# Mamba scan in held order: the second layer's weights made inside the scan loop, and the gate moved ahead of the scans of its slot

## The chip, the cores and the metric

The kernel runs on one core of one Trainium2 chip. The metric is device time in microseconds (us). The kernel before takes 9756.96 us, the median of three runs (9746.79 to 9757.15).

## The reference

The model is a chain of four blocks on a tensor of 4 batches, 96 channels and 64x64 positions. Blocks 0 and 2 are the ones that the change touches, and both are the same program (`mamba_fusion`) with other weights. Each has two Mamba layers and a fusion:

```python
seq = x.reshape(b, c, L).transpose(0, 2, 1)
for i in range(NLAYERS):                       # 2 layers
    seq = seq + _mamba_block(seq, ...)         # layernorm, in_w, conv of 4 taps, silu, xproj_w,
                                               # delta, A = -exp(A_log), scan, + Dp*xc, * silu(z), out_w
...
gp = relu(x.mean((2, 3)) @ gp_w.T + gp_b)      # one vector for each batch
out = einsum('oc,bchw->bohw', fus_w, cat(mamba_out, gp)) + fus_b
# batch norm of out, + residual
```

The scan is `h[t] = dA[t] * h[t-1] + dBx[t]` for 192 inner channels and 16 states, over L = 4096 positions, with `dA = exp(delta * A)` and `dBx = delta * B * xc`; `y` sums `h * C` over the states, adds `Dp * xc`, and is multiplied by `silu(z)`. That last multiplication is called the gate here. Block 1 is a state-space block in another form (`ssd`), block 3 a ConvNeXt block (`convnext`); neither is touched.

## The kernel before, in words

`mamba_fusion` works on two batches at once (a pair). A step is one pair, one layer (`sub` 0 or 1) and one chunk of 512 positions; there are 2 pairs x 2 layers x 8 chunks = 32 steps, in that order, so the second layer's weights are first needed in the ninth step. The 2 x 192 inner channels fill three blocks of 128 partitions (j = 0, 1, 2).

`Scan.run` cuts each step into 24 groups, eight for each j, and walks them with one loop variable n. One turn of that loop is called a slot, and the slot's number within its chunk a position (0 to 23). In slot n every stage works on another group, so many slots ahead or behind: `load` is five ahead (SP issues the loads of delta, and in one group of four also of delta times x, spread over the 16 states), `spread` one ahead (TensorE writes delta times x to a PSUM tile `bs`, two buffers; in the other groups ScalarE writes the exponentials there), `decay` and `product` two ahead (exponentials on ScalarE; one product on GpSimd for one group of four), `scan` in its own slot (on VectorE: one product of 128x1024, L369, in three groups of four, and then two scans of 128x512, L374), `after` one behind (GpSimd: hc = h times C, L381; ScalarE keeps the last state), `sums` three behind (TensorE: the sum over states to one PSUM bank `py` with a single buffer, L400). `front` (`mamba_front`) prepares the next step: layernorm, convolution, projections and the softplus, cut by `yield` into small parts that run one or two in a slot (`PACE`).

After the last group of a j, its gate `close` (L408) multiplies `py` by silu(z) on VectorE. It comes four slots after that group: at position 11 for j = 0, at position 19 for j = 1, and at position 3 of the next chunk for j = 2. Until it has read `py`, the first `sums` of the next j, in the same slot, can't start. `project` and `project_rest` follow one and two slots later.

The order of the work is written by hand: at the end of each slot the instructions of every engine, SP's DMA issues too, are tied behind the previous one of that engine, so that nothing in the loop is reordered:

```python
for ins in traced[start:]:
    ...
    self.tc.add_manual_dep(ins, last[ins.engine].name, IN_ORDER, reason="order")
```

Before the loop starts, `mamba_fusion` loads and prepares: selections, the first layer's weights, the whole front of the first step, sums of x for the fusion, then the second layer's weights (`mamba_weights(..., 1, ...)`, L494 to L534) and the fusion's (L629 to L655). On SP the second layer's weights are 26 issues, 16 of them for `w_a` (L527). The fusion's part turns the second layer's output weights by the fusion's matrix on TensorE (L638 to L645, PSUM tag `mm`) and makes the vector `gb`. Those instructions stand ahead of the loop's first ones; outside the loop the order is the scheduler's.

## Time and profile before

| what | value |
|---|---|
| median of three runs | 9756.96 us |
| the profiled execution's own time | 9748.23 us |
| its span, first to last instruction | 9746.5 us |
| block 0: first scan starts, last scan ends | 88.24, 3017.34 us |
| block 2: first scan starts, last scan ends | 6225.50, 9150.70 us |
| VectorE busy in 88 to 3018 us | 2733.29 of 2930 us |
| TensorE busy there, at a mean granted clock of 0.93 | 2510.75 us |
| GpSimd busy there | 2510.97 us |
| two products 24 slots apart (position 22 of the first and second chunk) | 170.77, 262.65 us |

The profile page gives the busy time of each engine over the whole span, then the costliest groups of instructions, each with the idle time of its engine just before them and with what ended that idle time. The timeline lists instructions by start; a bracket at a line's end tells how long the engine had been idle, and who released it. Matmul rows come in pairs of records for each float32 matmul, so `x4` is the two matmuls of one slot. `PEclk` and the clock of a window are shares of TensorE's full clock. VectorE is called DVE, TensorE PE, ScalarE ACT, and GpSimd POOL in the rows.

### The profile page before, as it was taken

To read this page: it belongs to the slowest core of one execution; us is meant where nothing else is said; L and a number is where in the kernel's file an instruction comes from. 1 tells how busy PE (TensorE), PEld (TensorE's weight loads), DVE (VectorE), ACT (ScalarE), POOL (GpSimd) and SP (SyncE) were. 2 spreads that over 40 slices of the span, in tenths; PEclk is the share of its full clock that TensorE was granted. 3 is DMA by queue.
4 is the path that set the end of the run, shared out by engine and by line. 5 is a ranking of instruction groups with operands and counts; after the bars stand their busy time and mean duration, and the time that the engine had idled before them with its cause. 6 is when DMAs were issued, how large, how long until landed. Compare 5 with 4: busy or idle time off the path is not lost. (4 is left out here: it accounts for less than half of the span.)

```text
span 9746.5 us, 109952 instructions
## 1 busy us (share of the span) xinstructions
PE 8319.4 (85%) x32896; PEld 3486.3 (36%) x32896; DVE 8080.8 (83%) x10870; ACT 5536.2 (57%) x10786; POOL 6860.0 (70%) x4573
## 2 busy tenths in 40 slices
PE   7888888888887998998898999688888888888678
PEld 1222222112123676776766777212222222222122
DVE  7999999999995666666666667699999999999887
ACT  5566666566664455455555545466666666666345
POOL 6888888888885555555555555588888888888511
PEclk8999999999997999999999999799999999999789
DMA  7777787777774222222322222677787877777653
GB/s 187 202 206 204 211 216 206 205 208 201 209 211 128 66 69 85 80 70 82 88 67 77 82 66 61 159 208 195 210 215 206 213 207 197 209 209 203 168 119 84
DMA packets 813856, 1531.94 MB, mean 157 GB/s; under 512 B 126893, under 2 KB 132425, under 8 KB 809802
## 3 DMA queue, kind: packets, MB, share of 16 engines
q1 hardware_dynamic: 810186, 1519.79, 58.6%
q8 instruction: 260, 4.26, 0.2%
q10 hardware_dynamic: 3072, 5.11, 0.1%
q14 instruction: 338, 2.77, 0.1%
HBM read 1229.28 MB, written 148.50 MB: 141 GB/s over the span
## 5 line engine op out<-in xcount | busy, mean ns | idle before, releaser
L381 POOL TENSOR_TENSOR hc<-hs,bc 128x1024 f32<-128x1024 f32 x1536 | 3611.0, 2356 | 742.8 <-DVE hs L374 399.9
L374 DVE TENSOR_TENSOR_SCAN hs<-da,carry,bs 128x512 f32<-128x512 f32 x2016 | 2470.8, 1267 | 119.6 <-DVE bs L369 1.4
L343 PE MATMUL bs<-du,seldu 64*128 64x512 f32 x4608 | 1467.8, 667 | 510.1 <-DVE hs L374 505.6
L400 PE MATMUL py<-hc,selsum 128*32 128x512 f32 x6144 | 1670.7, 651 | 261.5 <-DVE xz L408 180.6
L369 DVE TENSOR_TENSOR bs<-bs,bc 128x1024 f32<-128x1024 f32 x1152 | 1406.3, 1221 | 254.1 <-PE bs L343 233.1
L111 ACT ACTIVATE da<-da,w_a 128x512 f32<-128x512 f32 x2304 | 1517.1, 710 | 0.0
L343 PEld LDWEIGHTS bs<-du,seldu 64*128 64x128 f32 x4608 | 409.9, 193 | 1484.3 <-DVE hs L374 1190.2
L351 POOL TENSOR_TENSOR du<-du,bc 128x1024 f32<-128x1024 f32 x384 | 904.7, 2356 | 50.3 <-DMA du<-dg 50.3
L1032 DVE TENSOR_SCALAR seg<-dr,dac 128x128 f32<-128x128 f32 x1536 | 637.0, 448 | 290.0 <-PE y L1077 287.7
L1048 POOL TENSOR_TENSOR seg<-seg,cb 128x384 f32<-128x384 f32 x512 | 514.9, 1007 | 476.5 <-DVE cb L1047 409.0
L374 DVE TENSOR_TENSOR_SCAN hs<-bs,carry,du 128x512 f32<-128x512 f32 x672 | 819.0, 1260 | 0.0
L205 PE MATMUL pu<-h,w_conv 96*128 96x512 f32 (+3 forms) x2048 | 796.4, 624 | 1.4 <-POOL h L179 1.4
L111 ACT ACTIVATE bs<-da,w_a 128x512 f32<-128x512 f32 x768 | 528.7, 688 | 444.9 <-DVE hs L374 431.8
L983 PE MATMUL front<-pk,sconv 128*128 128x512 f32 x1536 | 753.8, 608 | 25.6 <-ACT z L971 21.7
L400 PEld LDWEIGHTS py<-hc,selsum 128*32 128x32 f32 x6144 | 222.4, 111 | 1504.8 <-issue 924.6
L1087 POOL TENSOR_TENSOR y<-y,xs 128x192 f32<-128x192 f32 x496 | 295.1, 595 | 605.1 <-DVE y L1086 590.1
L1100 ACT ACTIVATE y<-yz 128x192 f32<-128x192 f32 x512 | 186.1, 363 | 906.3 <-DVE yz L1099 905.3
L1052 POOL TENSOR_TENSOR xs<-pre,coef 128x576 f32<-128x576 f32 x512 | 597.9, 1172 | 53.4 <-ACT pre L116 25.3
L994 PE MATMUL front<-sconv,pk 128*128 128x192 f32 x3072 | 572.5, 330 | 57.1 <-DVE pre L999 51.9
L384 ACT COPY carry<-hs 128x2 f32<-128x2 f32 x1344 | 246.7, 184 | 514.2 <-DVE hs L374 513.8
L994 PEld LDWEIGHTS front<-sconv,pk 128*128 128x128 f32 x3072 | 496.7, 190 | 89.6 <-DVE pre L999 78.7
L1077 PEld LDWEIGHTS y<-xs,seg 128*128 128x128 f32 x3072 | 442.9, 206 | 144.2 <-issue 83.9
(229 smaller groups left out, 13743.1 us busy)
## 6 DMA issues: line engine op xcount, KB each, us to landing
da<-dd SPq DMA_DIRECT2D x3072, 256.0 KB
du<-dg SPq DMA_DIRECT2D x768, 256.0 KB
dr<-rows SPq DMA_DIRECT2D x256, 384.0 KB
bc<-rows SPq DMA_DIRECT2D x256, 256.0 KB
dd<-delta SPq DMA_DIRECT2D x192, 256.0 KB
dg<-du SPq DMA_DIRECT2D x192, 256.0 KB
pk<-xn SPq DMA_DIRECT2D x128, 384.0 KB
pk<-xn SPq DMA_DIRECT2D x128, 256.0 KB
```

The source lines that it names most:

```text
L111: self.last = self.scalar.activation(out, in_, func, **kw)
L205: nc.tensor.matmul(pu[r0:r1], lhsT=wt["conv"][:kk, tap, d0:d1], rhs=h[:kk, b, ds(tap, T)], start=(tap == 0), stop=(tap == 3),)
L343: nc.tensor.matmul(g["bs"][:, i], lhsT=self.sel["du"][rows, g["half"], g["q"]], rhs=g["made"]["du"][rows, g["j"]], start=True, stop=True,)
L351: self.tc.nc.gpsimd.tensor_tensor(g["du"], g["du"], self.b_or_c(g, 0), ALU.mult)
L369: nc.vector.tensor_tensor(dbx, dbx, self.b_or_c(g, 0), ALU.mult)
L374: nc.vector.tensor_tensor_scan(hs[:, i], da[:, i], dbx[:, i], init, ALU.mult, ALU.add)
L381: nc.gpsimd.tensor_tensor(g["hc"], hs, self.b_or_c(g, 1), ALU.mult)
L400: nc.tensor.matmul(py[rows], lhsT=self.sel["sum"][:, g["q"]], rhs=g["hc"][:, i], start=(g["q"] == 0), stop=(g["q"] == NQU - 1),)
L983: nc.tensor.matmul(p, lhsT=self.conv[:, i, DI + q * DST : DI + (q + 1) * DST], rhs=pk[:, i, ds(c * T, T)], start=(i == 0), stop=(i == 2),)
L994: nc.tensor.matmul(p, lhsT=pk[:, i, ds(c * Q, Q)], rhs=self.conv[:, i, :DI], start=(i == 0), stop=(i == 2),)
L1032: nc.vector.tensor_scalar(seg[:, h], g["pair"]["dr"][:, c % 2 * NH + h], made["dac"][:, n0 + h : n0 + h + 1], 0.0, ALU.subtract, ALU.min,)
L1052: nc.gpsimd.tensor_tensor(xs, x.to_broadcast([P, 3, NH, HD]), coef.to_broadcast([P, 3, NH, HD]), ALU.mult)
```

## The change

Three things are moved; nothing is computed otherwise.

- The second layer's and the fusion's weights are made by a generator, `other_weights`, handed to `run` as `later`. Its parts run one in a slot: fourteen in the slots of positions 0 to 13 of the second chunk (loads and preparation), and four in positions 8 to 11 of the third (the three turns of the output weights, and `gb`). In a slot they stand after the scans and the front's parts, and ahead of `sums`. They use the PSUM bank `po` (one buffer) in place of `mm`.
- In a slot with a gate, the gate stands between the slot's product and its two scans, instead of after the scans. All slots with a gate have a product.
- `mamba_weights` is a generator; for the first layer it is run through at once, where it was.

```diff
-    def scan(self, g):
+    def scan(self, g, gate):
...
             nc.vector.tensor_tensor(dbx, dbx, self.b_or_c(g, 0), ALU.mult)
+        if gate:
+            self.close(gate)
         hs = self.state.tile([P, GS, T], F32, name="hs", bufs=4)
...
-                (self.product, -2), (self.scan, 0),
+                (self.product, -2),
...
-            if (g := at(4)) and g["last"]:
-                self.close(g)
+            gate = (g := at(4)) and g["last"] and g
+            if g := at(0):
+                self.scan(g, gate)
+            elif gate:
+                self.close(gate)
...
+            if n in range(each, each + 14) or n in range(2 * each + 8, 2 * each + 12):
+                next(later, None)
             if g := at(3):
                 self.sums(g)
...
-    wts.append(mamba_weights(nc, k.act, k.ident, one, w, 1, one7))
...
+    def other_weights():
...
+        yield from mamba_weights(nc, k.act, k.ident, one, w, 1, wts[1])
...
+        for j in range(3):
+            pt = psum.tile([P, T], F32, tag="po", name="pt", bufs=1)[:C, :P]
+            nc.tensor.transpose(pt, wts[1]["out"][:, j], k.ident)
+            turned = work.tile([P, T], F32, tag="ua", name="turned", bufs=2)[:C, :P]
+            nc.scalar.copy(turned, pt)
+            pw = psum.tile([P, T], F32, tag="po", name="pw", bufs=1)[:, :C]
+            nc.tensor.matmul(pw, lhsT=turned, rhs=fus[:, 0], start=True, stop=True)
+            nc.scalar.copy(wts[1]["out"][:, j], pw)
+            yield
```

## The prediction

> **What bounds the kernel now.** I read the costliest groups on the page first, then the table by stretches, then the waits, then the timelines of SP, VectorE and TensorE. The chain of waits is of no use here: most of what it lists lies after 9150 us, in the last block.

> ```profile
> L369 DVE TENSOR_TENSOR bs<-bs,bc 128x1024 f32<-128x1024 f32 x1152 | 1406.3, 1221 | 254.1 <-PE bs L343 233.1
> ...
> 88.00:3018.00 2930.00, 2510.75 (x7915) 593.23 (x7914) 2733.29 (x2458) 1817.68 (x3377) 2510.97 (x1207) 0.93 0.77 205
> 6225.00:9151.00 2926.00, 2505.71 (x7915) 593.70 (x7914) 2733.20 (x2458) 1817.71 (x3377) 2510.51 (x1207) 0.93 0.78 205
> ...
> PE py L400 <- DVE xz L408: 180.6, 91, 3.2
> ```

> The third busy time is VectorE's: 93% of both scan loops, so VectorE sets their length, and only its gaps and the time before the first scan can be won. Its main wait is for `bs` from TensorE (233.1 us). TensorE in turn waits 180.6 us for the gate L408.

> The start of the first loop: SP issues weights while the loop's loads queue behind them.

> ```profile
> 56.69 0.32 SPq L246 DMA_DIRECT2D dg<-du  x1
> 57.10 0.59 SPq L512 DMA_DIRECT2D w_xproj<-in_L_xproj  x1
> ...
> 59.73 12.13 SPq L527 DMA_DIRECT2D w_a<-in_L_a  x16
> ...
> 73.94 2.51 SPq L326 DMA_DIRECT2D da<-dd  x4
> ...
> 86.90 1.23 DVE L369 TENSOR_TENSOR bs<-bs,bc 128x1024 f32<-128x1024 f32 x1 [12.64 <-PE bs L343]
> ```

> A usual chunk, at position 19 (gate of j = 1), first VectorE, then TensorE:

> ```profile
> 249.31 1.21 DVE L369 TENSOR_TENSOR bs<-bs,bc 128x1024 f32<-128x1024 f32 x1
> 250.62 2.45 DVE L374 TENSOR_TENSOR_SCAN hs<-da,carry,bs 128x512 f32<-128x512 f32 x2
> 252.99 0.67 DVE L408 TENSOR_TENSOR xz<-py,xz 128x512 f32<-128x512 f32 x1
> ...
> 262.65 1.23 DVE L369 TENSOR_TENSOR bs<-bs,bc 128x1024 f32<-128x1024 f32 x1 [2.93 <-PE bs L343]
> ```

> ```profile
> 249.44 2.04 PE L343 MATMUL bs<-du,seldu 64*128 64x512 f32 x4 [2.92 <-DVE hs L374]
> 253.80 1.92 PE L400 MATMUL py<-hc,selsum 128*32 128x512 f32 x4 [2.31 <-POOL hc L381]
> ...
> 261.48 1.13 PE L343 MATMUL bs<-du,seldu 64*128 64x512 f32 x4
> ```

> TensorE stands idle for 2.31 us until the gate ends at 253.66 (the hc named ends then too, but it is a later group's), is then busy without a break to 262.6, and VectorE waits 2.93 us at position 22. I followed this wait through all chunks: in 60 of 64 it is 1.97 to 3.02 us.

> The same chunk at position 11 (gate of j = 0):

> ```profile
> 217.69 1.23 DVE L369 TENSOR_TENSOR bs<-bs,bc 128x1024 f32<-128x1024 f32 x1
> ...
> 221.42 0.67 DVE L408 TENSOR_TENSOR xz<-py,xz 128x512 f32<-128x512 f32 x1
> ```

> ```profile
> 216.51 1.13 PE L343 MATMUL bs<-du,seldu 64*128 64x512 f32 x4
> 217.57 2.14 PE L215 MATMUL pz<-h,w_in 96*128 96x512 f32 x6
> 219.63 1.05 PE L400 MATMUL py<-hc,selsum 128*32 128x512 f32 x4
> ```

> Here the sums that the gate reads end at 220.69, 0.73 us before the gate as it stands, but 1.77 us after the product ends at 218.92. In 62 of 64 chunks they end after the product, 1.6 to 1.8 us.

> [...] one `bs` matmul record is 0.59 us at 228 us and 1.06 to 1.18 us at 250, and the windows from 249.5 to 259.7 show a clock of 0.50. [...] each `w_a` load is 1.5 KB, and between 62 and 70 us they fill 0.28 to 0.30 of the DMA engines at 2 to 4 GB/s. [...] `du` is issued by 77.74, and GpSimd, released by it, starts at 83.34.

> **The change part by part.** (1) *The start.* SP is rid of the issues from 57.10 to 73.94 (16.8 us), TensorE and ScalarE of the turned weights and `gb` (74.3 to 79.9), VectorE of 2.1 us of preparation. What is late next is the data. The first loads were issued from 73.94, and `du` of the second group released GpSimd at 83.34, 9.4 us later. Issued from 57.1 they release it at 66.5; the product of 2.35 us ends at 68.9, and the second group's scan starts near 69.0 instead of 91.64: 22.7 us. In block 2 SP is free at 197.4 + 6000 instead of 6212.24; 9.4 + 2.35 later is 6209.2 against 6228.33: 19.1. Sum **-42** (ends: -33, SP's 16.8 and 14.9 alone and a little, and -50).

> (2) *The same work in the loop.* VectorE gets the conv product 0.94, two memsets 0.22 each, `w_dd` 0.56 and the sign 0.19: 2.13 us a block, on the path. Behind `w_xproj`'s load, which waits for a memset, queue the loads of `da` five groups ahead; SP gets back by about three slots (11 us) before they are needed, so nothing. The `w_a` loads, 1.5 us of SP for the two in a slot, kept 0.29 of 16 engines busy for 0.76 us each, 3.5 engine-us; 16 of them over 30 us add 0.12 to a DMA share of 0.78: covered, 5 us a block if not. At positions 8 to 11 of the third chunk TensorE waits in place for ScalarE's copies: transposition 0.42, copy 0.26, product 0.74, or about 1.2 us each with a warm clock. Three of them stand ahead of the sums of j = 0, where TensorE is the late one: about 4 us a block. Sum **+12** for two blocks (4 to 25).

> (3) *The gate ahead of the scans.* Position 19: `py` was complete at 246.52, so the gate runs at 250.6 and ends near 251.3. TensorE, done with `bs` at 251.5, goes on without its idle 2.3 us[...]. Its chain (sums 1.92, pc 2.02, sums 1.92, po 2.1 cold; half of it warm) then ends between 257.4 and 259.5, its `bs` between 258.6 and 260.6, and VectorE arrives at 259.7. The 168 us found at position 22 shrink to some 18: **-150** (0 to -168). The scans of that slot start 0.67 later, but the gate no longer follows them: VectorE's sum is the same.
> Position 3: TensorE saves 1.3 us, and gets ahead until it waits for a scan at position 5. The waits for `bs` at positions 6 to 8 are 233.1 - 24 (the two starts) - 165 (position 22) = 44; **-40** (0 to -44).
> Position 11: VectorE itself now waits for the sums, with two scans queued behind. The distance is 1.77 us, less about 0.9 that TensorE got ahead, plus 0.5 that VectorE arrives earlier[...]: 1.5 us x 64 = **+96** (+64 to +120). The later slots only have to follow VectorE, which is later.
> Position 3 again: with a warm clock the sums end 1.2 us before the product, no wait. In 10 of 63 chunks they end 1.6 us after it; there TensorE was cold at positions 1 and 2 (273.4 to 280.2). [...] perhaps half of them are cold: 31 x 1.75 = **+54** (+17 to +110).
> Gate in all: -150 - 40 + 96 + 54 = **-40**.

> Sum: 9748.2 (the profiled execution; 9 below the median of the runs, inside their range) - 42 + 12 - 40 = 9678. I take 9680.

> **The rivals.** *The wait changes engines* (slower): VectorE pays at positions 3 and 11 (96 + 54), and the wait at position 22 stays, because what makes it is the cold clock and TensorE's row of sums, pc and po, not the gate. Then 9748 - 30 + 150 - 20 (positions 6 to 8) = 9848. It decides where under 1.3 us of the 2.6 us a chunk are released at position 22: (2.35 - 0.6 - 1.25) x 64 is the 30 that the start gives. For it: TensorE is cold there anyway. Against: its idle 2.31 us ends exactly with the gate.
> *A draw*: gate gains and gate waits cancel, and the start alone remains: 9748 - 30 = 9718. [...]
> *TensorE gets well ahead*: without its stops it is early at position 11 too, waits fall to 20 us in all: 9748 - 30 - 190 + 20 = 9548. Against: from 205 to 230 us it is busy without a gap.
> That nothing moves can be excluded: in the order of the changed program the gate stands between product and scans in every slot that has one, and the weights inside the loop.

> **How the numbers follow.** Forecast 0.62 (9640 to 9715), changed engines 0.14 (9750 to 9900), draw 0.14 (9690 to 9760), well ahead 0.10 (9520 to 9600). The range 9575 to 9780 leaves out most of the last and half of the second case. A measurement here tells 0.2% (20 us) from no change: faster by more 0.77 (0.60 + 0.07 + 0.10), within 0.07, slower 0.16.

> **What would show it.** In the profile after: the first scan near 64 us and the second loop's some 20 us nearer to its front; L369's wait for `bs` falling from 233 us to below 80; TensorE's wait for L408 nearly gone; a new wait of L410 (the gate) for `py` of 100 to 200 us, at positions 11 and some of 3; idle 2 to 3 us at position 22 gone. I am wrong if the gate's wait exceeds 250 us, or position 22 still waits over 1.3 us, or `da` arrives late in the second chunk.

## The result, and the profile after

The changed kernel takes 9619.41 us, the median of four runs (9609.21 to 9629.35), against 9754.06 us for the kernel before (9746.79 to 9757.15, four runs). The ratio is 0.9863, with a 95% interval of 0.9847 to 0.9878: 135 us faster. The prediction said 9680 us, 68 us faster than the profiled execution of the kernel before. The profiled execution after took 9615.6 us, its span is 9613.6 us, 132.9 us less than before.

First the page's groups of the kernel after (busy time and mean of one, then the idle time just before them and what ended it), next its waits, and then the table by stretches, one line for each scan loop:

```profile
L402 PE MATMUL py<-hc,selsum 128*32 128x512 f32 x6144 | 1619.3, 633 | 34.4 <-DVE xz L410 28.9
L369 DVE TENSOR_TENSOR bs<-bs,bc 128x1024 f32<-128x1024 f32 x1152 | 1396.9, 1213 | 47.8 <-PE bs L343 37.3
```

```profile
DVE xz L410 <- PE py L402: 175.7, 111, 5.1
```

```profile
61.00:2956.00 2895.00, 2503.80 (x7929) 595.12 (x7929) 2720.66 (x2463) 1817.91 (x3388) 2517.91 (x1207) 0.94 0.80 209
6131.00:9018.00 2887.00, 2487.32 (x7929) 591.78 (x7927) 2719.66 (x2463) 1817.53 (x3386) 2517.84 (x1208) 0.95 0.81 209
```

The product's wait for `bs` has fallen from 233.1 to 37.3 us, and TensorE's wait for the gate from 180.6 to 28.9. In their place VectorE has a wait that it did not have: the gate L410 stands 175.7 us for `py`. Of that 168.4 lie inside the two loops: I added the brackets by position and found 116.2 at position 11 (62 of 64 chunks, 1.8 each) and 52.1 at position 3 (47 of 62, 42 of them over 0.5 us). VectorE is busy for 94% of each loop now.

The start, SP and then VectorE:

```profile
55.88 0.32 SPq L246 DMA_DIRECT2D dg<-du  x1
56.25 1.83 SPq L326 DMA_DIRECT2D da<-dd  x3
```

```profile
59.87 1.23 DVE L369 TENSOR_TENSOR bs<-bs,bc 128x1024 f32<-128x1024 f32 x1 [7.77 <-PE bs L343]
61.21 2.33 DVE L376 TENSOR_TENSOR_SCAN hs<-da,bs 128x512 f32<-128x512 f32 x2
...
66.62 2.34 DVE L376 TENSOR_TENSOR_SCAN hs<-bs,du 128x512 f32<-128x512 f32 x2 [2.51 <-POOL du L351]
```

The loads of `da` follow at once, at 56.25 instead of 73.94, and the first scan starts at 61.21 instead of 88.24. What is late next is what the prediction named: the second group's scan waits for `du` by way of GpSimd, whose loads have all landed at 64.02, and starts at 66.62.

A usual chunk at position 19 and after it, then positions 3 and 11 of other chunks, all VectorE:

```profile
319.47 1.21 DVE L369 TENSOR_TENSOR bs<-bs,bc 128x1024 f32<-128x1024 f32 x1
320.59 0.68 DVE L410 TENSOR_TENSOR xz<-py,xz 128x512 f32<-128x512 f32 x1
321.18 2.44 DVE L376 TENSOR_TENSOR_SCAN hs<-da,carry,bs 128x512 f32<-128x512 f32 x2
323.54 1.21 DVE L369 TENSOR_TENSOR bs<-bs,bc 128x1024 f32<-128x1024 f32 x1
...
329.60 1.21 DVE L369 TENSOR_TENSOR bs<-bs,bc 128x1024 f32<-128x1024 f32 x1
...
349.60 0.69 DVE L410 TENSOR_TENSOR xz<-py,xz 128x512 f32<-128x512 f32 x1 [0.48 <-PE py L402]
...
376.41 1.23 DVE L369 TENSOR_TENSOR bs<-bs,bc 128x1024 f32<-128x1024 f32 x1
379.46 0.69 DVE L410 TENSOR_TENSOR xz<-py,xz 128x512 f32<-128x512 f32 x1 [1.81 <-PE py L402]
380.06 2.44 DVE L376 TENSOR_TENSOR_SCAN hs<-da,carry,bs 128x512 f32<-128x512 f32 x2
```

At position 19 the gate waits for nothing, and the product of position 22 (329.60) has no bracket, where before it had 2.93. At position 11 the gate waits 1.81 us, and both scans stand behind it.

Look closely at 319.47 to 321.18. The gate starts 0.09 us *before* the product's recorded end (320.68), the scan 0.09 us before the gate's. In the lines of before the scan started 0.10 us *after* the product's end (250.52 to 250.62). That small thing returns below.

### The profile page after: what moved, and what is told of

The parts are those of the page before. It is cut to its first block, busy times and chain, and to the rows that moved or that the text cites. A ratio compares the mean times of both kernels' runs of the same rounds, so it can differ in the third digit from the quotient of the medians.

```text
span 9613.6 us, 109902 instructions
## 1 busy us (share of the span) xinstructions
PE 8280.0 (86%) x32896; PEld 3476.0 (36%) x32896; DVE 8048.5 (84%) x10870; ACT 5532.2 (58%) x10786; POOL 6872.2 (71%) x4573
## 3 DMA queue, kind: packets, MB, share of 16 engines
q8 instruction: 260, 4.26, 0.2%
## 5 line engine op out<-in xcount | busy, mean ns | idle before, releaser
L343 PE MATMUL bs<-du,seldu 64*128 64x512 f32 x4608 | 1488.7, 682 | 683.3 <-DVE hs L376 676.8
L402 PE MATMUL py<-hc,selsum 128*32 128x512 f32 x6144 | 1619.3, 633 | 34.4 <-DVE xz L410 28.9
L369 DVE TENSOR_TENSOR bs<-bs,bc 128x1024 f32<-128x1024 f32 x1152 | 1396.9, 1213 | 47.8 <-PE bs L343 37.3
L343 PEld LDWEIGHTS bs<-du,seldu 64*128 64x128 f32 x4608 | 409.0, 196 | 1687.9 <-DVE hs L376 1272.5
```

Of the source, the lines that this page charges most:

```text
L343: nc.tensor.matmul(g["bs"][:, i], lhsT=self.sel["du"][rows, g["half"], g["q"]], rhs=g["made"]["du"][rows, g["j"]], start=True, stop=True,)
L369: nc.vector.tensor_tensor(dbx, dbx, self.b_or_c(g, 0), ALU.mult)
L402: nc.tensor.matmul(py[rows], lhsT=self.sel["sum"][:, g["q"]], rhs=g["hc"][:, i], start=(g["q"] == 0), stop=(g["q"] == NQU - 1),)
```

## The experiments

Block 1, which nothing touches, takes a different time in each kernel: from the last scan of block 0 to its own last instruction, 3114.6 us before, 3104.4 after, and between 3098.5 and 3128.0 in the kernels below. I don't know why. Where a difference of 20 us matters, I therefore add up the two scan loops alone, from first scan to last: 5854.3 us before, 5780.6 after. "Product waits" and "gate waits" are the sums, inside these loops, of VectorE's idle time just before such instructions, also where it is too short for a bracket (under 0.15 us): product waits 230.1 us before and 32.2 after, gate waits 0 and 168.4. Each ratio is to executions of the kernel before that were taken along with the kernel in question; their medians lie between 9750.8 and 9760.3 us.

### One half alone: the gate

The kernel before, with the gate put between product and scans. The weights stay ahead of the loop.

```diff
-                (self.product, -2), (self.scan, 0),
+                (self.product, -2),
...
-            if (g := at(4)) and g["last"]:
-                self.close(g)
+            gate = (g := at(4)) and g["last"] and g
+            if g := at(0):
+                self.scan(g, gate)
...
```

> The kernel before with the gate alone moved between product and scans; the weights stay ahead of the loop. Theory: both gains are separate; the two starts (59 us by the profiles) are not won, and the loops lose 74 us plus the 12 us that the weights cost inside them: 9754 - 86 = 9668, with a first scan at 88 us and a wait of the gate for py of about 170 us. Rival: the loops run faster because the start left TensorE's clock and the buffers in another state, not because of the gate: then the loops keep their 2929 and 2925 us and the time is near 9754.

Measured: 9658.71 us (9624.04 to 9660.97), ratio 0.9905 (0.9888 to 0.9921).

```profile
DVE xz L410 <- PE py L402: 150.3, 102, 3.7
DVE bs L369 <- PE bs L343: 39.1, 62, 11.4
```

Inside the loops the product waits are 24 us, none of them at position 22, so the wait at position 22 is the gate's doing and not the cold clock's alone: the rival "the wait changes engines" falls. The gate alone is worth about 95 us (9753.31 - 9658.71), not the 40 of the prediction. (The profiled execution is the fastest of the four; the lines are its own.)

### The other half alone: the weights

The kernel after, with the gate behind the scans again:

```diff
-                self.scan(g, gate)
-            elif gate:
+                self.scan(g, None)
+            if gate:
                 self.close(gate)
```

> The changed kernel with the gate put back behind the scans of its slot. Theory: only the two starts are won, 59 us, less some 12 us for the weights' work inside the loops: 9754 - 47 = 9707, with waits for bs of 200 us or more in the loops again (position 22). Rival (the start makes the loops faster): near 9630.

Measured: 9724.39 us (9712.65 to 9750.82), ratio 0.9973 (0.9964 to 0.9983): 29 us, where the prediction's terms -42 and +12 give 30. (The 47 expected here had counted the starts to the first scan, and block 1's 10 us with them.)

```profile
DVE bs L369 <- PE bs L343: 232.7, 179, 7.8
PE py L402 <- DVE xz L410: 174.6, 88, 3.6
```

Both waits of before are there again. The halves add up to 124 us of the 135. What the weights cost inside the loop stands in the third chunk, here 98.2 us long in both blocks against 92.8 and 91.9 before; the second is 0.5 longer. Together 12.8 us. TensorE of the kernel after shows where:

```profile
284.81 0.31 PE L662 MATMUL pt<-ident,w_out 128*96 128x128 f32 x1
286.86 0.46 PE L666 MATMUL pw<-fus,turned 96*128 96x96 f32 x2 [1.74 <-ACT turned L664]
287.25 1.92 PE L402 MATMUL py<-hc,selsum 128*32 128x512 f32 x4
```

The copy of 0.26 us that TensorE waits for is queued on ScalarE behind a table load of 1.28 and a copy of 0.59. So this turn takes 2.4 us, not 1.2 (the one before it took 0.9), the sums behind it are at half clock (a granted clock of 0.50 from 287.21 to 290.63; 1.92 us for about 1.05, called cold below), and the gate waits 5.13 us there.

### What the wait at position 11 costs

The kernel after, with only the gates of j = 0 behind their scans:

```diff
+            late = gate and gate["j"] == 0
             if g := at(0):
-                self.scan(g, gate)
-            elif gate:
+                self.scan(g, None if late else gate)
+            if gate and (late or not g):
                 self.close(gate)
```

> The changed kernel, but the gate of j = 0 (position 11) stands behind its scans as before; those of j = 1 and 2 stay between product and scans. Theory: the 116 us that VectorE waits at position 11 go, some 12 us of the bubble between product and scan come back, and TensorE, which is late there anyway, makes no new wait: 9619 - 104 = 9515. Rival: TensorE is what sets the pace there, so that the wait comes back as waits for bs at positions 12 to 16: 9600 to 9620.

Measured: 9507.89 us (9499.31 to 9528.58), ratio 0.9753 (0.9738 to 0.9767).

```profile
DVE xz L410 <- PE py L402: 43.8, 50, 3.7
```

Inside the loops the gate waits fall from 168 to 36.5 us, 31.6 of it at position 3; product waits are 34.8 us, for 32.2. The wait at position 11 is a real loss: nothing fills it, and when it goes the product waits only 2.6 us longer. But these waits are 129 us shorter in all, and the loops only 116.5. The 13 us between are about what was expected to come back when the 64 gates of j = 0 no longer part a product from its scan: net of waits their slots take 4.32 us (median) from product to product, as before, against 4.20 after.

### Sums ahead of the front's parts

The other way to end the gate's wait: `sums` is issued before the parts of `front`, in every slot.

```diff
+            if g := at(3):
+                self.sums(g)
             for _ in range(PACE[slot] if slot < len(PACE) else 0):
                 next(ahead, None)
...
-            if g := at(3):
-                self.sums(g)
```

> The changed kernel with one more move: in each slot the sums stand ahead of the front's parts on TensorE instead of behind them. Theory: the sums that the gate reads end 2.1 us earlier at position 10, and about 2 us earlier at position 2, so the 175 us of the gate's waits nearly vanish; some 30 us come back as waits for bs: 9619 - 130 = 9490. Rival: TensorE as a whole is late at positions 3 to 11, so the front's parts now come late instead, and the time stays near 9600.

Measured: 9548.98 us (9534.98 to 9558.84), ratio 0.9791 (0.9776 to 0.9805). All gate waits are gone, but product waits rise to 97 us, and block 1 took 24 us more than after. The time lies between the two numbers: the waits moved in part.

### Is there a gap that the gate fills?

After the sums of waits, VectorE's loops were still shorter than the prediction's "VectorE's sum is the same" allows. The suspicion is the 0.10 us between product and scan. In this kernel the gate stands between the two scans of its slot:

```diff
-        if gate:
-            self.close(gate)
         hs = self.state.tile([P, GS, T], F32, name="hs", bufs=4)
         for i in range(GS):
...
+            if i and gate:
+                self.close(gate)
```

> The gate stands between the two scans of its slot. Theory (the gate ahead of both scans gains about 0.19 us a slot because it fills the gap between the product and the first scan that depends on it): that gain is lost, a gate slot net of its waits is near 4.26 us at position 19 again and not 4.07 (+36 us over both loops). The wait of the gate starts 1.25 us later: at position 11 it falls from 1.8 to about 0.55 us (116 to 34 us), at position 3 from 52 to some 12 us. TensorE is let go 1.25 us later, some 15 us of the product's waits come back. Sum 9619 + 36 - 82 - 40 + 15 = 9548 us. Rival (there is no gap to fill, the 36 us came from elsewhere): gate slots stay near 4.07 us, time near 9512 us.

Measured: 9608.61 us (9600.42 to 9611.57), ratio 0.9843 (0.9826 to 0.9859): neither number. VectorE at position 19:

```profile
324.11 1.21 DVE L369 TENSOR_TENSOR bs<-bs,bc 128x1024 f32<-128x1024 f32 x1
325.42 1.28 DVE L376 TENSOR_TENSOR_SCAN hs<-da,carry,bs 128x512 f32<-128x512 f32 x1
326.62 0.67 DVE L410 TENSOR_TENSOR xz<-py,xz 128x512 f32<-128x512 f32 x1
327.20 1.27 DVE L376 TENSOR_TENSOR_SCAN hs<-da,carry,bs 128x512 f32<-128x512 f32 x1
328.39 1.21 DVE L369 TENSOR_TENSOR bs<-bs,bc 128x1024 f32<-128x1024 f32 x1
...
335.23 1.23 DVE L369 TENSOR_TENSOR bs<-bs,bc 128x1024 f32<-128x1024 f32 x1 [0.70 <-PE bs L343]
```

The theory of the gap holds. The scan again starts 0.10 us after the product that it reads, and from product to product the slot takes 4.28 us (324.11 to 328.39), against 4.07 after (319.47 to 323.54) and 4.26 before. Gate waits fall to 26.6 us, more than expected. What ate the gain is the product: its waits are 106.5 us, 68.1 of them at position 22. The gate ends 1.38 us later after the product's start (3.18 for 1.80) and position 22 waits 1.04 us more (66.5 over 64 chunks): three quarters of what holds TensorE at the gate come back there. Block 1 took 13 us more than after.

### Sums first in two slots only

The kernel after, with the sums ahead of the front's parts at positions 2 and 10, the slots before the two gates that wait:

```diff
+            early = n % each in (2, 10)
+            if early and (g := at(3)):
+                self.sums(g)
             for _ in range(PACE[slot] if slot < len(PACE) else 0):
                 next(ahead, None)
...
-            if g := at(3):
+            if not early and (g := at(3)):
                 self.sums(g)
```

> Only at positions 2 and 10, the slots before the gates of j = 2 and j = 0, do the sums stand ahead of the front's parts on TensorE; the gate is ahead of the scans everywhere. Theory (the gate waits because a front's matmuls stand ahead of the last sums there, and moving them in every slot cost product waits and chunks of 93.5 us): gate waits fall from 168 us to some 10, product waits stay near 32: 9619 - 158 = 9461, about 9464 us. Rival (the front's parts are then late themselves, whichever slot it is): product waits near 90 us come back, 9515 to 9550 us.

Measured: 9515.35 us (9511.31 to 9522.09), ratio 0.9750 (0.9736 to 0.9765), the rival's number.

```profile
DVE bs L369 <- PE bs L343: 99.8, 148, 7.8
```

No gate waits, but of these product waits 44.5 us are now at position 6, in 49 chunks, where the kernel after had 1.6 in 5.

And the gate of j = 0 after its scans, with the sums early at position 2 only:

```diff
+            early = n % each in (2,)
```

> The gate of j = 0 after its scans as in the earlier run, and the sums ahead of the front's parts at position 2 alone. Theory: the 31.6 us that the gate waits at position 3 in that run go, 9508 - 32 = 9476 us; the 64 gates of j = 0 do not fill the gap ahead of their scans, so it stays some 12 us above the kernel that moves the sums at both positions. Rival (position 3 then waits for something else, or the front is late): 9505 us or more.

Measured: 9519.37 us (9516.64 to 9534.03), ratio 0.9757 (0.9742 to 0.9771). The gate's 31.6 us at position 3 are gone, product waits rose from 34.8 to 68.6, 28.1 of them at position 6; the loops take 5663.0 us against 5664.1. That is the rival's outcome: nothing is gained. Position 11's wait is a matter of order, since it went for good in two ways; position 3's is not: TensorE itself is late in these slots, and VectorE meets it at one place or at the next.

### Why TensorE is late at position 3

In the kernel after, the gate of position 3 waits only after a cold clock: in 47 of the 51 chunks whose mean clock over the 11 us before was under 0.95, and in none of the other 11. TensorE at the turn of a chunk, first of the kernel before, then of the one with the gate of j = 0 after its scans:

```profile
270.53 1.07 PE L400 MATMUL py<-hc,selsum 128*32 128x512 f32 x8
274.13 2.08 PE L343 MATMUL bs<-du,seldu 64*128 64x512 f32 x4 [2.54 <-DVE hs L374]
```

```profile
512.88 1.07 PE L402 MATMUL py<-hc,selsum 128*32 128x512 f32 x8
517.26 2.08 PE L343 MATMUL bs<-du,seldu 64*128 64x512 f32 x4 [3.32 <-DVE hs L376]
519.27 2.07 PE L396 MATMUL py<-xz,w_dd 128*128 128x512 f32 x2
521.27 1.92 PE L402 MATMUL py<-hc,selsum 128*32 128x512 f32 x4
```

Between positions 23 and 0 TensorE waits for a scan to free a `bs` buffer. Through all chunks the median of that idle time is 2.46 us in the kernel before, 3.25 in the kernel after: freed from its stops at the gates, TensorE gets to this wait sooner (3.25 us also with the gate alone moved, 2.46 with the weights alone). A cold stretch followed in 11 of 62 chunks before, in 51 of 62 after.

To test that the idle time is the cause, five matmuls with zero weights, which add nothing to `py`, are put in the slot of position 23 of the kernel with the gate of j = 0 after its scans (the tile of zeros and its memset are left out here):

```diff
+            if n % each in (23,) and (g := at(3)):
+                for _ in range(5):
+                    nc.tensor.matmul(
+                        g["made"]["py"][:QUART], lhsT=self.sel["zero"], rhs=g["hc"][:, 0],
+                        start=False, stop=False,
+                    )
```

> The kernel with the gate of j = 0 after its scans, plus five matmuls with zero weights in the slot of position 23 of every chunk (they add nothing to py), where TensorE stands idle for 2.5 to 3.3 us in every chunk and after which it is at half clock in 79% of the slots of position 1. Theory (the gate's wait at position 3 is made by the cold clock, and the cold clock by that idle time): position 1 stays warm in nearly all chunks, the gate's wait at position 3 falls from 31.6 us to below 5, the waits for bs at position 6 stay near 2: 9508 - 30 = about 9478 us. Rival (the clock goes cold all the same, or the wait comes from the front's parts): position 3 keeps 25 us or more, and the extra 2.6 us of TensorE a chunk are late at the next bs: 9508 us or more.

Measured: 9493.76 us (9477.26 to 9506.70), ratio 0.9738 (0.9722 to 0.9754). TensorE, and the stretch from 505 to 530 us (the clock is the third number from the end):

```profile
511.45 1.05 PE L402 MATMUL py<-hc,selsum 128*32 128x512 f32 x4
512.33 3.17 PE L499 MATMUL py<-hc,selzero 128*32 128x512 f32 x7
...
516.72 1.13 PE L343 MATMUL bs<-du,seldu 64*128 64x512 f32 x4
517.78 1.13 PE L396 MATMUL py<-xz,w_dd 128*128 128x512 f32 x2
```

```profile
505.00:530.00 25.00, 25.00 (x83) 6.47 (x80) 24.39 (x23) 13.06 (x27) 23.05 (x12) 1.00 0.72 184
```

No chunk of 62 is cold there any more, and the same `bs` takes 1.13 instead of 2.08 us. The gate's wait at position 3 falls from 31.6 us in 46 chunks to 12.0 in 32, the loops from 5664.1 to 5647.9. (The medians differ by 14 us, and the runs of the two kernels overlap; the argument rests on the clock and on the loops.) So here the idle time makes the cold clock (51 of 62 chunks after the change, none with it filled), and the cold clock more than half of the wait (31.6 to 12.0 us). The 12 us left are more than the 5 expected; they stand at a full clock, and their cause is open.

The same five matmuls in the kernel with early sums at positions 2 and 10:

> The kernel with the sums ahead of the front's parts at positions 2 and 10, plus the same five matmuls at position 23. Theory: the waits for bs at position 6, 44.5 us in 21 chunks, are the same cold clock's, moved there from the gate of position 3; with the idle time filled they go, while the gates still wait for nothing: 9515 - 42 = about 9473 us. Rival (position 6 waits since the front's parts stand behind the sums): 44 us stay there, 9515 us or more.

Measured: 9476.96 us (9472.59 to 9480.97), ratio 0.9716 (0.9702 to 0.9731).

```profile
DVE bs L369 <- PE bs L343: 58.7, 96, 7.8
```

Position 6 falls from 44.5 to 13.2 us, and no gate waits. The two loops fall from 5681.2 to 5641.2 us. It is the fastest of all kernels here, 142 us below the change as it was made, by the medians.

## Why the prediction was right, and where it was not

The direction and the places were right, the size is half of what came. Its terms against the traces, in us; starts are counted to the second group's scan:

| term | predicted | measured |
|---|---|---|
| the two starts | -42 | -43 (25.0 and 18.4) |
| product waits | -190 | -198 (position 22: -160; 6 to 8: -33) |
| gate waits | +150 | +168 (position 11: +116; 3: +52) |
| the weights' waits on TensorE | +8 | in the two rows above, about 10 |
| VectorE's time in the loops without these waits | +4 | -50 |
| block 1, not touched | 0 | -10 |
| sum | -70 | -133 |

*The start* was right. SP's 16.8 us of issues went, and most of the time from the loads' issue to the data stayed: 7.8 us (56.25 to 64.02), where before it was 9.3 (73.94 to 83.19). The issues' own spans end before the data has landed: those of `du` end at 59.35, its data is there at 64.02.

*Weights in the loop*: 12 predicted, 12.8 measured with the old gate. With the new gate the second and third chunks together, from first scan to first scan, are 5.5 and 8.1 us longer than two mean chunks of the same loops, 13.6 in all. The parts were less well sized: VectorE's added instructions take 3.0 us a block instead of 2.13 (the product that makes `w_dd` took 1.27 us in the loop and 0.56 ahead of it), and a turn waits for ScalarE up to 1.74 us.

*The gate.* Position 22 followed the gate as read (its wait before was 161 us in the trace, 168 in the prediction). That half of TensorE's chain would be warm was my estimate; in the chunks shown, half clock lasts 10.24 us before (249.52 to 259.76) and 3.41 after (321.35 to 324.76). Position 11 was mis-sized by a fifth, 1.8 us for 1.5; a gate that waits starts 0.05 us after the end of the sums (median of 111). Position 3 came right in its sum by luck: 31 waits of 1.75 us were forecast, and 47 of 1.1 came. That half of the chunks would be cold was my estimate. Left out of it was that the change itself lengthens TensorE's idle time at the turn of the chunk, from 2.46 to 3.25 us, so that 51 of 62 chunks were cold and not half of them.

*The step that failed* is "VectorE's sum is the same". It is the -50. The loops, from the second group's scan on, can be taken apart by pairs of neighbours on VectorE, waits of product and gate left out:

- A scan behind the product that it reads starts 131 ns (median of 1152 cases before) after that one's end. A scan behind a scan, a gate behind a scan and a scan behind a gate overlap by 82 to 84 ns. With the gate between them, the pair that depends is no longer adjacent. In 190 slots the gap goes, -23 us, and the 81 gates that wait for nothing overlap the product, -7.
- The product waits 181 times instead of 392, short waits counted too. A product that does not wait overlaps the scan before it by 0.08 us: -17.
- The products themselves are shorter by 9 us in all (a waiting one lasts 1.233 us, another 1.209 to 1.215), the scans by 3. Why, no run tests.
- Against these stand +6 of the weights' instructions and +4 of the gates, which last longer in their new place. About 2 us are left over.

The first part is shown by experiment: with the gate between the scans the gain is gone, and with the gate of j = 0 behind them it is gone for those 64. The second is a sum over the trace. What makes the two kinds of pair differ, by 0.21 us, no run here shows.

*Block 1's* 10 us are no effect of the change that any run shows. In the two half kernels it took 3115 us, as before.

Of the rivals, "the wait changes engines" was excluded by the gate alone, and "a draw" by the result. "TensorE well ahead" (9548) and the forecast (9680) lie about equally far from the result in time, but the rival's mechanism did not come: the gate's waits that it supposed gone are there.

## What to carry to other kernels

When an instruction is moved up on the busiest engine to release another one, price both the wait that it may take on itself and the pairs that it parts: between an operation and the one that reads its result a small independent one cost less here than its own duration (net of waits, a slot of the kernel after takes 3.69 us from product to product without a gate, the median of 514, and 4.07 at position 19 with one of 0.68 us). If two changes of order only move a wait from one slot to the next (here from position 3 to position 6), order is not the cause, and the late engine's own pace, its clock included, has to be looked at. Releasing an engine can make its idle time gather at the next wait, and there it can become long enough to cost the clock (here 3.25 us for 2.46, and half clock behind it in 51 of 62 chunks for 11).

## What was not expected of the hardware

Idle time of TensorE of 3.25 us (median) at one place was followed by half clock in 51 of 62 chunks, of 2.46 us in 11 of 62, and with the idle time filled by matmuls on zero weights in none of 62. In the traces of both kernels half clock followed, but for 20 of 2979 windows, where about 1.75 us or more of idle time fell into one window of the measured 3.413 us. The five matmuls take some 3.4 us of TensorE in every chunk (512.33 to 516.72, less about 1.0 for the slot's own sums), and still made the kernel faster: with the early sums by 38 us by the medians, 40 in the two loops.

A scan right behind the product that it reads costs 0.21 us more than one behind an instruction that it does not read, at a duration of 1.2 us for the product. 1152 such pairs are in this kernel, and only 192 of them have a gate to part them.
